# Transposing the first group of a row tile's exponentials ahead of the last multiplication of the tile before it

## The chip, the cores and the metric

One core of a Trainium2 chip runs the kernel. The metric is the device time of one execution in microseconds (us). Engines are named as in the profile: PE is the matrix engine (TensorE), PEld its weight loads, DVE the vector engine, ACT the scalar engine, POOL is GpSimd, SP the queue that starts most of the DMAs.

## What is computed

Two graph layers over 2708 nodes with 256 features. Only the attention of the first layer is touched by the change:

```python
for n in range(2):                        # STEPS
    probs = softmax((Xa @ W1.T @ W2.T) @ (Xa @ W3.T).T)
    mask  = the fewest largest probs of a row that sum to over 0.9
    A     = probs * mask;  A = A / A.sum(-1)
    Xf = R @ Xf                           # R: the given adjacency, with the identity added, by row sums
    Xa = A @ Xa
    Z  = Z + Xf @ U1[n].T + Xa @ U2[n].T
x = layernorm(x + (layernorm(x + Z) * g + b))
# then a second layer: masked attention with 4 heads, residual, layernorm
```

A is 2708 x 2708 and is never stored; it is made and used one row tile at a time.

## The kernel before

Rows are cut into 22 tiles, `rows = [128] * 16 + [110] * 6`. For a product A @ X the same 22 tiles are the blocks of the inner dimension, put into six `groups` of equal width: four groups of four tiles, and then one of four and one of two (the 110-wide ones).

For each of the two steps, `step` (L995) goes through the row tiles. A row tile t has its masked exponentials e (rows on partitions, 2708 columns) ready in the dictionary `ready`. `weigh` (L202) multiplies them by the current X. Since the inner dimension must lie on partitions, e is transposed first, group by group. `turned(n)` (L208) transposes up to four blocks on PE into a PSUM tile `tr` (L212) and copies it on ACT to an SBUF tile `eT` (L218). The multiplications of group n (L227) take eT as the stationary operand and add into one PSUM tile, `att`, of which there is one buffer (`ps_at`, bufs=1). Each fp32 multiplication is two matmul instructions in the profile, so a group of four blocks is 8 of them and the last group of two blocks is 4; a transpose is one. In the text below, "group 0" to "group 5" are these multiplications, and "the transposes of group n" their preparation.

`weigh` keeps one group ahead, within a row tile: it transposes group 0, and then for each n it transposes group n+1, multiplies group n, and calls `between(n)`. After the last group `between` (L1006) first reads `att` out with a scaled ACT copy into `xa` (L1010). Every `between` then calls `slot`.

A `slot` (L980) is the place where other work is woven in. It moves every search that is going on by one stage (`going`), starts a new one where `begin` says so, moves every piece of following work by one stage (`doing`), and then issues up to `spend` block multiplications of the two adjacency products R @ Xf (`walks`, L824, matmuls of L863). In step 0 `spend` is 0; in step 1 it is 7, 6, 7, 7, 6, 7 over the six groups.

A `search` (L811) makes e and its mask for one row tile. Its first stage issues the score matmuls of two of three column pieces (L631) and their exponentials on ACT (L635), the second stage the third piece. In step 0 it takes 6 stages. In step 1 it takes 13: stages 3 to 6 hold counts over e on ACT (L656), stage 7 a bound on DVE (L704 to L725), then come candidates, sorting and the replacement of ties, and the 13th masks e in place on DVE (L805). The search of tile t+3 is started in the slot after the last group of tile t, so that its 13th stage is issued in the slot right ahead of its own first transposes. There are three e buffers.

The stretch of code is under `tc.manual_schedule`: PE, ACT, DVE and POOL get their instructions in the order in which the Python code issues them. Between the steps there is a run of 13 slots, each with 7 block multiplications, which brings the searches of tiles 0, 1 and 2 of step 1 forward. The adjacency products have 968 block multiplications in all; the slots of step 1 and of that run issue up to as many, and what is issued in one slot is not left for a later one.

Of the kernel before, what the change touches and what calls it, by code (L numbers as in the profile page):

```python
# [8 lines left out]
F32 = mybir.dt.float32  # L9
# [7 lines left out]
P = 128  # L17
# [27 lines left out]
def kernel(  # L45
# [16 lines left out]
    nc = tc.nc  # L62
    N, D = x.shape
# [4 lines left out]
    NT = (N + P - 1) // P  # L68

    rows = [P] * 16 + [110] * 6  # L70
    assert sum(rows) == N and len(rows) == NT
    off = [sum(rows[:t]) for t in range(NT + 1)]
    chunks = [(c, min(CHUNK, N - c)) for c in range(0, N, CHUNK)]
    HT = NT // 2
    groups = []
# [29 lines left out]
    ident = const.tile([P, P], F32, name="ident")  # L105
# [67 lines left out]
    def share(g, tr):  # L173

        span, m = spans[g], rows[spans[g][0]]
        k = len(span) * H
        nc.tensor.transpose(
            tr[:k, 0, :m],
            s_src[:m, span[0] : span[-1] + 1, :].rearrange("p t h -> p (t h)"), ident[:m, :m],
        )  # L180
        nc.scalar.activation(line[:k, :m], tr[:k, 0, :m], AF.Exp, scale=1.0 - NEG_SLOPE)
        nc.sync.dma_start(shared[g], line[:k, :m])
# [16 lines left out]
            for _ in range(2)  # L199
        ]  # L200

    def weigh(acc, e, m, value, pool, ps, copies, between=None):  # L202

        def turned(n):  # L208
            grp = groups[n]
            tr = ps.tile([P, 4, P], F32, name="tr")  # L210
            for q, t in enumerate(grp):
                nc.tensor.transpose(  # L212
                    tr[: rows[t], q, :m], e[:m, off[t] : off[t + 1]], ident[:m, :m]
                )
            eT = pool.tile([P, 4, P], F32, name="eT")
            copy = copies[n % len(copies)]
            k = rows[grp[0]]
            copy(eT[:k, : len(grp), :m], tr[:k, : len(grp), :m])  # L218
            return eT

        ahead = turned(0)
        for n, grp in enumerate(groups):
            eT = ahead
            if n + 1 < len(groups):
                ahead = turned(n + 1)
            for q, t in enumerate(grp):
                nc.tensor.matmul(  # L227
                    acc, eT[: rows[t], q, :m], value(t),
                    start=(t == 0), stop=(t == NT - 1),
                )  # L230
            if between:
                between(n)


    def general_layer0():
        with ExitStack() as l0:
# [25 lines left out]
            tpp = l0.enter_context(tc.tile_pool(name="tpp", bufs=4))  # L262
            adjp = l0.enter_context(tc.tile_pool(name="adjp", bufs=2))
            ps_lg = l0.enter_context(tc.tile_pool(name="ps_lg", bufs=2, space=PSUM))
            ps_tr = l0.enter_context(tc.tile_pool(name="ps_tr", bufs=2, space=PSUM))
# [34 lines left out]
            def scores(s, t):  # L300

                m = rows[t]
                lo, hi = s * DA, (s + 1) * DA
                e = ep.tile([P, N], F32, name="e")
                for c0, w in chunks:
                    lg = ps_lg.tile([P, CHUNK], F32, name="lg")
                    nc.tensor.matmul(
                        lg[:m, :w], qT[lo:hi, off[t] : off[t + 1]], kT[lo:hi, c0 : c0 + w],
                        start=True, stop=True,
                    )  # L310
                    nc.scalar.copy(e[:m, c0 : c0 + w], lg[:m, :w])
                nmx = small.tile([P, 1], F32, name="nmx")
                nc.vector.tensor_reduce(nmx[:m], e[:m], axis=AX.X, op=ALU.max, negate=True)
                z = small.tile([P, 1], F32, name="z")
                nc.scalar.activation(e[:m], e[:m], AF.Exp, bias=nmx[:m], accum_out=z[:m])
                tau = small.tile([P, 1], F32, name="tau")
                nc.vector.tensor_scalar(tau[:m], z[:m], TOP_P, None, op0=ALU.mult)
                return e, tau
# [89 lines left out]
            def attend(t, e, rden, cur, dst):  # L408

                m = rows[t]  # L410
                ac = ps_ac.tile([P, CHUNK], F32, name="ac")
                weigh(ac[:m, :D], e, m, lambda j: cur[: rows[j], j, 0:D],
                      tpp, ps_tr, [nc.scalar.copy])
                nc.scalar.activation(dst, ac[:m, :D], AF.Copy, scale=rden[:m])

            def walk(s, t, dst):
# [52 lines left out]
            for s in range(STEPS):  # L469
                cur = xe if s == 0 else xa1  # L470
                ahead = scores(s, 0)
                for t in range(NT):
                    m = rows[t]
                    e, tau = ahead
                    if t + 1 < NT:
                        ahead = scores(s, t + 1)
# [6 lines left out]
                    rden = top_p(t, e, tau)  # L483
# [10 lines left out]
    def fast_layer0(ep, adjp):  # L494
# [3 lines left out]
        heldp, finp, rowp, w0, keep, sortp, tpp, wk = (  # L498
            l0.enter_context(tc.tile_pool(name=name, bufs=bufs))
            for name, bufs in (  # L500
                ("heldp", HELD), ("finp", 2), ("rowp", 2), ("w0", 1), ("keep", 1),
                ("sortp", 1), ("tpp", 3), ("wk", 1),
            )
        )
        ps_lg, ps_wk, ps_at, ps_tr = (
            l0.enter_context(tc.tile_pool(name=name, bufs=bufs, space=PSUM))
            for name, bufs in (("ps_lg", 2), ("ps_wk", 1), ("ps_at", 1), ("ps_tr", 2))
        )
# [69 lines left out]
        tr = ps_tr.tile([P, 4, P], F32, name="tr")  # L578
# [3 lines left out]
        for c in range(DC):  # L582
            tr = ps_tr.tile([P, 4, P], F32, name="tr")
# [227 lines left out]
        def search(s, t):  # L811

            e, z, tau = yield from scores(s, t)
            if s:
                seen = yield from survey(t, e, z, tau)
                src, rest = bound(t, e, z, tau, *seen)
            else:
                src, rest = e, tau
            yield
            cand = yield from candidates(s, t, src)  # L820
            yield
            ready[t] = e, (yield from settle(s, t, e, cand, rest))
# [148 lines left out]
        ready, held = {}, {}  # L971
# [3 lines left out]
        def advance(parts):  # L975
            for g in list(parts):
                if next(g, parts) is parts:
                    parts.remove(g)

        def slot(spend, begin=None):  # L980

            advance(going)
            if begin and begin[1] < NT:
                going.append(search(*begin))
                next(going[-1])
            advance(doing)
            owed[0] += spend
            while owed[0] > 0:
                owed[0] -= 1
                if next(stream, True):  # L990
                    break

        ahead = []

        def step(s, cur, spend):  # L995
            for t in range(NT):
                m = rows[t]
                e, rden = ready.pop(t)
                ac = ps_at.tile([P, CHUNK], F32, name="att")
                if s and t == NT - 2:  # L1000
                    share(0, ps_tr.tile([P, 4, P], F32, name="tr"))
                if s and t == NT - 1:
                    ahead.extend(room(ep))
                    spread(0, ahead)

                def between(n):  # L1006
                    last = n == len(groups) - 1
                    if last:
                        xa = heldp.tile([P, D], F32, name="xa1")
                        nc.scalar.activation(xa[:m], ac[:m, :D], AF.Copy, scale=rden)  # L1010
                        if s and t in c3:
                            nc.gpsimd.dma_start(c3[t][:m], xa[:m])
                            stored.add(t)
                        elif s:
                            held[t] = xa
                        else:
                            doing.append(after_attention0(t, xa))
                    slot(spend[n], (s, t + 3) if last else None)

                weigh(ac[:m, :D], e, m, lambda j: cur[: rows[j], j, 0:D],  # L1020
                      tpp, ps_tr, [nc.scalar.copy], between)

        def layer1_weights():

# [26 lines left out]
        for grp in groups:  # L1051
            k = rows[grp[0]]
# [13 lines left out]
        with tc.manual_schedule(engines=engines):  # L1066
            for n in range(10):
                slot(0, (0, n // 4) if n in (0, 4, 9) else None)
                for t in range(n * NT // 10, (n + 1) * NT // 10):
                    terms1(t, x_turned[:, :, off[t] : off[t + 1]])  # L1070
            layer1_weights()
            step(0, xm, [0] * len(groups))
            while doing:
                slot(SPEND_BETWEEN)


            for t in range(3):
                for n in range(6):
                    slot(SPEND_BETWEEN, None if n else (1, t))
                    if t == 2:  # L1080
                        break
            step(1, ba, SPEND_1)
            owed[0] = 0
            while doing:
                slot(NT)
# [234 lines left out]
```

## Time and profile before

| | |
|---|---|
| median of 3 runs | 1656.84 us (1656.59 to 1657.43) |
| the profiled execution: time, span | 1657.21 us, 1655.3 us |
| step 0 of the attention, by the first and last multiplications of it | 78 to 468 us |
| run of slots between the steps | 468 to 530 us |
| step 1 | 530 to 1252 us |
| last following work of layer 0, and layer 1 | 1252 to 1655 us |
| PE busy over the span | 1577.3 us, 95% |
| DVE, ACT, POOL busy | 74%, 45%, 26% |

A row of the costliest groups gives line, engine, operation, what it writes and reads, and the count; then the busy time, the mean length of one in ns, and the idle time of its engine just before it with what ended that. A row of the timeline gives the start, the length of a merged run of equal instructions, and in square brackets the idle time before it with its releaser. A row of the waits gives who waited for whom: us in total, times, and the longest.

### The profile page before, as it was taken

The page shows a single profiled execution, that of the slowest core. Times are in us where ns is not written, and L with a number is a line of the kernel's source. Part 1 is how long each engine was busy: PE and PEld are TensorE (multiplying, and loading weights), DVE is VectorE, ACT ScalarE, POOL GpSimd, SP SyncE. Part 2 cuts the span into 40 slices and gives each one's busy share as a digit, 9 for nine tenths or more (in the row PEclk, how much of TensorE's full clock was granted, in tenths as well). Part 3 has the DMA queues.
Part 4 walks back from the last instruction along what each step waited for, and adds up shares of the span by engine and source line. Part 5 has one row for each costly group of instructions (what it writes and reads, how often), then busy time and mean ns, then how long its engine had stood idle before and what let it go on. Part 6 is the DMA issues. An engine that isn't in the chain of part 4 may idle for free. (4 is left out here: it accounts for less than half of the span.)

```text
span 1655.3 us, 23835 instructions
## 1 busy us (share of the span) xinstructions
PE 1577.3 (95%) x8029; PEld 1035.8 (63%) x8029; DVE 1229.6 (74%) x3682; ACT 742.3 (45%) x1263; POOL 430.1 (26%) x908
## 2 busy tenths in 40 slices
PE   7999999999999999999999999999997999999894
PEld 3476667666677887787778877887773222222332
DVE  3676667666508877876888888987873999899795
ACT  3433444343335555455455655556524344243231
POOL 2200000000022223222225554455433030420313
PEclk9999999999999999999999999999997999999997
DMA  7200000000024333233333433433354333432231
GB/s 196 69 9 15 9 9 11 9 9 8 12 68 121 90 90 98 80 83 78 80 90 97 111 106 99 111 100 91 90 132 143 109 92 97 123 88 80 79 84 32
DMA packets 172493, 128.26 MB, mean 77 GB/s; under 512 B 44342, under 2 KB 161804, under 8 KB 172362
## 3 DMA queue, kind: packets, MB, share of 16 engines
q1 hardware_dynamic: 166442, 115.87, 26.0%
q0 software_dynamic: 3648, 9.26, 1.8%
q10 hardware_dynamic: 2272, 1.52, 0.3%
q8 instruction: 65, 1.06, 0.3%
q14 instruction: 66, 0.54, 0.1%
HBM read 111.78 MB, written 13.46 MB: 76 GB/s over the span
## 5 line engine op out<-in xcount | busy, mean ns | idle before, releaser
L218 ACT COPY eT<-tr 128x512 f32<-128x512 f32 (+5 forms) x264 | 137.7, 539 | 252.0 <-PE tr L212 251.5
L227 PE MATMUL att<-xm,eT 128*128 128x256 f32 (+3 forms) x968 | 229.3, 381 | 17.4 <-ACT eT L218 17.4
L656 ACT ACTIVATE junk<-e,minus,rth 128x2708 bf16<-128x2708 f32 (+1 forms) x88 | 232.8, 2646 | 14.6 <-POOL rth L688 13.7
L227 PE MATMUL att<-ba,eT 128*128 128x256 f32 (+3 forms) x968 | 232.9, 381 | 5.1 <-ACT eT L218 4.9
L1241 PE MATMUL acc<-pt,v 128*64 128x512 f32 (+3 forms) x1056 | 229.3, 555 | 5.7 <-DVE pt L1233 4.5
L863 PE MATMUL walk<-xe,blk 128*128 128x257 f32 (+3 forms) x968 | 223.8, 382 | 1.9 <-DVE xf L877 1.8
L863 PE MATMUL walk<-xm,blk 128*128 128x256 f32 (+3 forms) x968 | 221.8, 380 | 0.0
L1233 DVE SCALAR_TENSOR_TENSOR pt<-e,tj,blk 128x1024 f32<-128x1024 f32 (+3 forms) x176 | 186.5, 1117 | 29.3 <-PE acc L1248 12.5
L863 PEld LDWEIGHTS walk<-xe,blk 128*128 128x128 f32 (+3 forms) x968 | 177.3, 185 | 46.7 <-issue 13.7
L227 PEld LDWEIGHTS att<-xm,eT 128*128 128x128 f32 (+3 forms) x968 | 171.2, 186 | 44.7 <-ACT eT L218 22.2
L863 PEld LDWEIGHTS walk<-xm,blk 128*128 128x128 f32 (+3 forms) x968 | 177.8, 186 | 32.9 <-issue 4.9
L227 PEld LDWEIGHTS att<-ba,eT 128*128 128x128 f32 (+3 forms) x968 | 171.0, 186 | 32.6 <-ACT eT L218 10.2
L635 ACT ACTIVATE e<-lg 128x1024 f32<-128x1024 f32 (+1 forms) x132 | 121.0, 921 | 131.6 <-PE lg L631 131.3
L736 DVE MAX8 cand<-e 128x8 f32<-128x170 f32 (+1 forms) x352 | 89.7, 323 | 114.4 <-ACT e L635 114.3
L1241 PEld LDWEIGHTS acc<-pt,v 128*64 128x64 f32 (+1 forms) x1056 | 72.8, 138 | 158.3 <-issue 112.0
L212 PEld LDWEIGHTS tr<-ident,e 128*128 128x128 f32 (+3 forms) x968 | 113.6, 139 | 45.5 <-PE lg L631 14.5
L212 PE MATMUL tr<-ident,e 128*128 128x128 f32 (+3 forms) x968 | 139.4, 270 | 0.9 <-DVE e L805 0.5
L1171 ACT ACTIVATE blk<-blk 128x1024 f32<-128x1024 f32 (+3 forms) x66 | 63.1, 956 | 165.9 <-DMA blk<-in_adjT_dram 159.5
L1248 PE MATMUL acc<-pt,sb 128*32 128x512 f32 (+3 forms) x1056 | 123.6, 548 | 0.0
L1233 DVE SCALAR_TENSOR_TENSOR pt<-r,tj,blk 128x1024 f32<-128x1024 f32 (+1 forms) x88 | 110.6, 1314 | 8.2 <-issue 5.5
L736 DVE MAX8 cand<-scr 128x8 f32<-128x97 f32 (+1 forms) x616 | 101.7, 244 | 0.0
L877 DVE TENSOR_TENSOR xf<-walk,xe 128x257 f32<-128x257 f32 (+1 forms) x22 | 9.4, 426 | 112.4 <-PE walk L863 112.4
(197 smaller groups left out, 1941.0 us busy)
## 6 DMA issues: line engine op xcount, KB each, us to landing
blk<-in_adjT_dram SPq DMA_DIRECT2D x32, 704.0 KB
blk<-in_adjT_dram SPq DMA_DIRECT2D x32, 512.0 KB
blk<-in_adjT_dram SPq DMA_DIRECT2D x48, 330.0 KB
blk<-in_adjT_dram SPq DMA_DIRECT2D x32, 320.0 KB
blk<-in_adjT_dram SPq DMA_DIRECT2D x12, 605.0 KB
blk<-in_adjT_dram SPq DMA_DIRECT2D x12, 440.0 KB
blk<-in_adjT_dram SPq DMA_DIRECT2D x18, 283.6 KB
c<-cs POOLq DMA_DIRECT2D x32, 128.0 KB, 2.0
```

The costliest lines, as they stand in the source:

```text
L212: nc.tensor.transpose(tr[: rows[t], q, :m], e[:m, off[t] : off[t + 1]], ident[:m, :m])
L218: copy(eT[:k, : len(grp), :m], tr[:k, : len(grp), :m])
L227: nc.tensor.matmul(acc, eT[: rows[t], q, :m], value(t), start=(t == 0), stop=(t == NT - 1),)
L635: nc.scalar.activation(halves[:m, :, c0 : c0 + w], lg[:m, :, :w], AF.Exp, accum_out=zp[:m, n : n + 1],)
L656: nc.scalar.activation(junk[:m], e[:m], func, scale=rth, bias=minus1[:m], accum_out=acc)
L736: nc.vector.max(cand[:, n, :], src[:m, n * size : min(N, (n + 1) * size)])
L863: nc.tensor.matmul(ac[:m, :w], blk[: rows[j], j - j0, :m], cur[: rows[j], j, 0:w], start=(j == 0), stop=(j == NT - 1),)
L877: nc.vector.tensor_add(xf[:m], ac[:m, : D + 1], xe[:m, t, :])
L1171: nc.scalar.activation(bar, bar, AF.Sign)
L1233: nc.vector.scalar_tensor_tensor(pt[:k, :gw], r[h // 2][:k, h % 2, :gw], tj[:k, j, h : h + 1], mask, op0=ALU.max, op1=ALU.mult,)
L1241: nc.tensor.matmul(acc[h // 2][c][q * FO : (q + 1) * FO, :w], v[j][:k, h - 1 + q, :], pts[h - 1 + q][:k, c0 : c0 + w], **at,)
L1248: nc.tensor.matmul(acc[2][c][h * 32 : (h + 1) * 32, :w], sb[:k, j, h : h + 1].to_broadcast([k, 32]), pts[h][:k, c0 : c0 + w], **at,)
```

## The change

`turned` is taken out of `weigh` and becomes a function of its own that is given the e tile. `weigh` is given the transposed first group instead of making it, asks a function `turn_next` for each next group, and returns the one it got last. In `step`, `turn_next(6)` of tile t is group 0 of tile t+1. So the four transposes of that group and their copy are issued ahead of the multiplications of group 5 of tile t, not after the slot that follows these. Because e of tile t+1 must then be ready one slot earlier, every search starts one slot earlier (after group 4), and the run of slots between the steps has two slots more. The version of the first layer that is only run for inputs that the fast one can't do (`general_layer0`) is adapted and keeps its order.

```diff
-    def weigh(acc, e, m, value, pool, ps, copies, between=None):
-        def turned(n):
...
-        ahead = turned(0)
+    def turned(e, m, n, pool, ps, copy):
+        grp = groups[n]
+        tr = ps.tile([P, 4, P], F32, name="tr")
+        for q, t in enumerate(grp):
+            nc.tensor.transpose(
+                tr[: rows[t], q, :m], e[:m, off[t] : off[t + 1]], ident[:m, :m]
+            )
+        eT = pool.tile([P, 4, P], F32, name="eT")
+        k = rows[grp[0]]
+        copy(eT[:k, : len(grp), :m], tr[:k, : len(grp), :m])
+        return eT
+
+    def weigh(acc, ahead, m, value, turn_next, between=None):
         for n, grp in enumerate(groups):
-            eT = ahead
-            if n + 1 < len(groups):
-                ahead = turned(n + 1)
+            eT, ahead = ahead, turn_next(n + 1)
             for q, t in enumerate(grp):
                 nc.tensor.matmul(
                     acc, eT[: rows[t], q, :m], value(t),
...
             if between:
                 between(n)
+        return ahead
...
         def step(s, cur, spend):
+            first = None
             for t in range(NT):
                 m = rows[t]
-                e, rden = ready.pop(t)
+                e, rden = ready[t]
...
-                    slot(spend[n], (s, t + 3) if last else None)
-
-                weigh(ac[:m, :D], e, m, lambda j: cur[: rows[j], j, 0:D],
-                      tpp, ps_tr, [nc.scalar.copy], between)
+                    slot(spend[n], (s, t + 3) if n == len(groups) - 2 else None)
+
+                def turn_next(n):
+                    u = t + n // len(groups)
+                    if u == NT:
+                        return None
+                    return turned(ready[u][0], rows[u], n % len(groups), tpp, ps_tr, nc.scalar.copy)
+
+                first = weigh(
+                    ac[:m, :D], first or turn_next(0), m,
+                    lambda j: cur[: rows[j], j, 0:D], turn_next, between,
+                )
+                ready.pop(t)
...
             for t in range(3):
                 for n in range(6):
                     slot(SPEND_BETWEEN, None if n else (1, t))
-                    if t == 2:
+                    if (t, n) == (2, 2):
                         break
```

More of the change, by code (lines that the diff above doesn't have):

```diff
@@ L200, in room @@
         ]
-    def weigh(acc, e, m, value, pool, ps, copies, between=None):
-        def turned(n):
[L209 to L219, printed above, removed]
-        ahead = turned(0)
+    def turned(e, m, n, pool, ps, copy):
[10 more added lines that the diff above has]
+    def weigh(acc, ahead, m, value, turn_next, between=None):
         for n, grp in enumerate(groups):
-            eT = ahead
-            if n + 1 < len(groups):
-                ahead = turned(n + 1)
+            eT, ahead = ahead, turn_next(n + 1)
             for q, t in enumerate(grp):
@@ L411, in attend @@
                 ac = ps_ac.tile([P, CHUNK], F32, name="ac")
-                weigh(ac[:m, :D], e, m, lambda j: cur[: rows[j], j, 0:D],
-                      tpp, ps_tr, [nc.scalar.copy])
+                def turn_next(n):
+                    return turned(e, m, n, tpp, ps_tr, nc.scalar.copy) if n < len(groups) else None
+                weigh(ac[:m, :D], turn_next(0), m, lambda j: cur[: rows[j], j, 0:D], turn_next)
                 nc.scalar.activation(dst, ac[:m, :D], AF.Copy, scale=rden[:m])
@@ L1017, in between, with turn_next @@
                             doing.append(after_attention0(t, xa))
-                    slot(spend[n], (s, t + 3) if last else None)
-                weigh(ac[:m, :D], e, m, lambda j: cur[: rows[j], j, 0:D],
-                      tpp, ps_tr, [nc.scalar.copy], between)
+                    slot(spend[n], (s, t + 3) if n == len(groups) - 2 else None)
+                def turn_next(n):
+                    u = t + n // len(groups)
[7 more added lines that the diff above has]
+                ready.pop(t)
         def layer1_weights():
```

## The prediction

> **What bounds the kernel now.** I read the busy times by stage first, then PE's waits in each stage, then the timeline of PE where a row tile ends and the next begins. The windows give the stretch, its length, and busy time of PE, PEld, DVE, ACT, POOL, then the granted clock.
>
> ```profile
> 78.00:468.00 390.00, 371.70 (x1851) 269.48 (x1850) 249.76 (x920) 155.17 (x356) 31.66 (x95) 1.00 0.03 10
> ...
> 530.00:890.00 360.00, 357.20 (x1733) 286.36 (x1732) 282.12 (x1070) 192.75 (x243) 96.15 (x232) 1.00 0.33 87
> 890.00:1252.00 362.00, 359.14 (x1780) 289.23 (x1779) 299.21 (x1072) 198.21 (x379) 176.79 (x350) 1.00 0.39 103
> 1252.00:1275.00 23.00, 10.64 (x32) 5.53 (x32) 13.19 (x18) 10.14 (x38) 11.12 (x13) 0.59 0.55 166
> ```
>
> PE sets the pace of both steps: it is idle for 18.3 of 390 us in step 0 and 5.7 of 722 us in step 1, while DVE has 36% and 20% to spare. PE's waits in 78 to 468 us, and then in 530 to 1252 us:
>
> ```profile
> PE att L227 <- ACT eT L218: 17.4, 21, 1.0
> ```
> ```profile
> PE att L227 <- ACT eT L218: 4.9, 20, 0.4
> ```
>
> Nearly all the idle time is one wait, once per row tile: a multiplication waits for the ACT copy of its transposed group. PE's timeline shows which one (step 0, then step 1):
>
> ```profile
> 201.30 1.99 PE L631 MATMUL lg<-junk,qT 64*128 64x512 f32 x8
> 203.22 1.09 PE L212 MATMUL tr<-ident,e 128*128 128x128 f32 x8
> 205.18 1.99 PE L227 MATMUL att<-xm,eT 128*128 128x256 f32 x8 [0.87 <-ACT eT L218]
> 207.10 0.82 PE L631 MATMUL lg<-junk,qT 64*128 64x330 f32 x4
> ...
> 208.13 0.60 PE L212 MATMUL tr<-ident,e 128*128 128x128 f32 x4
> 208.57 1.89 PE L227 MATMUL att<-xm,eT 128*128 128x256 f32 x8
> 210.30 1.88 PE L922 MATMUL tr<-u_sb,xT 128*128 128x512 f32 x4
> ...
> 216.57 2.76 PE L227 MATMUL att<-xm,eT 110*128 110x256 f32 x12
> 219.25 1.99 PE L631 MATMUL lg<-junk,qT 64*128 64x512 f32 x8
> ```
> ```profile
> 819.60 1.02 PE L227 MATMUL att<-ba,eT 110*128 110x256 f32 x4
> 820.55 1.99 PE L631 MATMUL lg<-kT,qT 64*128 64x512 f32 x8
> ...
> 826.91 1.04 PE L212 MATMUL tr<-ident,e 128*128 128x128 f32 x8
> 828.18 1.99 PE L227 MATMUL att<-ba,eT 128*128 128x256 f32 x8 [0.24 <-ACT eT L218]
> 830.11 0.83 PE L631 MATMUL lg<-kT,qT 64*128 64x330 f32 x4
> ```
>
> The run of eight transposes is groups 0 and 1 of the new tile, with nothing else to cover the copy of group 0; everywhere else four transposes are followed by eight multiplications without a gap. ACT's timeline says why the wait is longer in step 0:
>
> ```profile
> 202.53 1.02 ACT L635 ACTIVATE e<-lg 128x1024 f32<-128x1024 f32 x1 [0.66 <-PE lg L631]
> ...
> 203.55 1.02 ACT L635 ACTIVATE e<-lg 128x1024 f32<-128x1024 f32 x1
> ...
> 204.54 1.07 ACT L218 COPY eT<-tr 128x512 f32<-128x512 f32 x2
> ...
> 219.36 0.47 ACT L1010 ACTIVATE xa<-att,rden 128x256 f32<-128x256 f32 x1 [2.17 <-PE att L227]
> ```
>
> The two exponentials of the search that this slot starts stand ahead of the copy. In step 1 the slot's block multiplications follow the scores, so they are done by then and only the copy itself shows.
>
> **What the Trainium skill says.** "Perfetto Trace Analysis", section Tensor Engine Instruction: PE's end times are estimated. The trace agrees (the transposes at 208.13 are 0.60 long, the next run starts 0.44 later), so I count from start to start, not the gaps. "TensorE: Matmul & The Clock Gate", Step-by-step: matmuls keep program order, only weight loads are drawn ahead; the trace shows no L227 passed by later work, so each entry's wait stops all behind it. The same page, What's actually happening: PE falls to half clock after an idle window of about 3.4 us. The waits are under 1 us and the clock is 1.00 in both steps (0.59 only in 1252 to 1275), so filling them wins no clock. "PSUM — Partial Sum Buffer", Engine vs sequencer instructions: ScalarE's queue is strictly in order; the copy at 204.54 starts at the end of the second exponential, as it says.
>
> **The change part by part.** *Entry, step 0.* Before, from the starts: groups 4 and 5 together take 219.25-216.57 = 2.68, the scores 203.22-201.30 = 1.92, eight transposes with group 0 and its wait 207.10-203.22 = 3.88; sum 8.48. After, the order is group 4, scores, four transposes, group 5, third score piece, four transposes, group 0. Four transposes take 208.57-208.13 = 0.44, a free group of eight 210.30-208.57 = 1.73, a group 5 alone ahead of scores 820.55-819.60 = 0.95, which is 0.08 over half of 1.73; I add this 0.08 to group 4 also, as scores now follow it. So 1.81+1.92+0.44+0.95+0.44+1.73 = 7.29 (the third piece is the same in both). The gain is 1.19 us, for the 19 entries whose slots start a search (tiles 1 to 19): 22.6. The entries of tiles 20 and 21 have no scores; their wait is small (0.29 of idle time at each in PE's timeline) and 0.3 each is taken: step 0 gives 23.2.
>
> *Entry, step 1.* Before: group 4 1.73, group 5 0.95, eight transposes with group 0 830.11-826.91 = 3.20; sum 5.88. After: 1.81+0.95+0.44+0.44+1.73 = 5.37. Scores and block multiplications are the same. The gain is 0.51, for 20 entries 10.2; tile 21's, where the mask is late by 0.5 today, 0.3. Step 1 gives 10.5. The first tile of each step keeps its wait.
>
> *What is late next: the read-out.* `att` has one buffer, so group 0 also waits for xa, now with four transposes less between; behind group 0 all of PE would queue. Count from the start L of the scores in step 0. ACT's exponentials end at L+3.24 (204.54-201.30), the copy of the next group 0 takes 0.59 (591 ns, mean of its group; L+3.83), and xa follows, 0.47: L+4.30. PE is back for group 0 at 1.92+0.44+0.95+0.76+0.44 = L+4.51 (0.76 is the third piece, 207.10 to 207.86 in PE's timeline). So 0.2 is spare: priced at nothing, with 0.3 x 19 = 6 us as the other end if ACT runs half a microsecond late. In step 1 seven block multiplications (about 3 us) lie between as well; no cost. The copy itself now has group 5, the third piece and four transposes of cover, 2.1 us; the next copy (group 1) follows the third exponential and has all of group 0, 1.7 us.
>
> *The searches one slot earlier.* All stages move together: PE's scores, ACT's counts, POOL's small steps, DVE's passes; each queue holds the same work in nearly the same order, and no DMA is added. What counts is that the mask is done at the entry.
>
> ```profile
> 820.41 3.02 DVE L805 SCALAR_TENSOR_TENSOR e<-scr,fact,e 128x2708 f32<-128x2708 f32 x1
> ```
>
> It ends at 823.43, and PE reads e at 826.91: 3.5 us spare. From the slot before to the entry PE now has the two transposes of group 5 (about 0.22) and the multiplications of group 4 (1.73) where it had group 5 (0.95), so 1.0 more. Cost nothing; queued behind a late mask would be the whole of PE.
>
> *Two more slots.* 14 block multiplications come before step 1 and are missing in its last tile: the sum of PE's work is the same. Gain or loss: at most 2 us either way (DVE waits in that run are 1.8 us today; the last tile has less to fill with, but its copies lie under 1.73 of multiplication). Zero.
>
> *The end of layer 0.* 1252 to 1275 is a chain that starts from the last xa. It moves as a whole, and layer 1 behind it; within 2 us either way as finishing work falls into other slots. Zero.
>
> *Sum.* 23.2+10.5 = 33.7. I keep back 1.5 for the small spare at the read-out: 32.2. The profiled execution took 1657.21 (its span of 1655.3 and 1.9 around it), 0.4 over the median, which is within the runs shown. 1657.2-32.2 = 1625.0.
>
> **Rivals.** *Only part (15%).* Either the read-out becomes the releaser in step 0, or the shorter runs cost more at each change of operation than I read. The gaps as the profile counts them are 17.4+4.9 = 22.3, which gives 1635; the read-out 0.5 us late (0.3 waited, 19 times) gives 1631. For it: 0.2 us of spare is little. Against: no work of ACT in the code stands between the copy and xa in step 0.
>
> *No change (3%).* The wait returns elsewhere, for instance DVE becomes the limit: 1657. Against: DVE has 36% and 20% spare. That the order is not kept is as good as excluded, since the timeline follows the code.
>
> *Slower (5%): the read-out behind the exponentials.* If ACT reached xa only after all three exponentials of a search (1.02+1.02+0.72 from ACT's timeline), it would come 2.8 us late, of which 0.2 is spare: 2.6 x 19 = 49 us in step 0, against a gain of 33.7: 1672. It decides from 2.0 us late (1.8 x 19 = 34). For it: strict order on ACT and one `att` buffer. Against: xa is issued ahead of the third, and the first two are fed by scores that PE now runs before group 5.
>
> **How the numbers follow.** As forecast, 1620 to 1630: 75%, with the two bounds of 2 us each and the read-out. Part of it: 15%. Better than 1620: 2%. No change 3%, slower 5%. The range from 1619 to 1637 leaves about 1 in 10 out, and what I have not thought of. About 0.2% (3.3 us) is what a measurement of this kernel can tell from no change: faster 0.92, same 0.03, slower 0.05.
>
> **What would show it.** PE's waits in step 0 should hold almost nothing for eT (the two first tiles' entries at most), and no new row "PE att <- ACT xa" of more than a microsecond or two; the timeline should read 8, scores, 4 transposes, 4, scores, 4 transposes, 8. Step 0 should last about 367 us, the run between the steps some 6 us longer (14 block multiplications, 0.43 each) and step 1 some 17 shorter. A wait of transposes for DVE e L805, several times, would make the searches' step wrong; a longer 1252 to 1275 stretch the end's.

## The result, and the profile after

| | before | after |
|---|---|---|
| median of 4 runs each, us | 1657.01 (1656.59 to 1657.43) | 1627.03 (1626.03 to 1628.40) |
| profiled execution: time, span | 1657.21, 1655.3 | 1626.46, 1624.7 |
| PE busy over the span | 1577.3 us | 1566.4 us |

The ratio is 0.982, with a 95% interval of 0.9803 to 0.9837. The change makes the kernel 30.0 us faster; the forecast was 32.2 us and a time of 1625.0.

The stages, from the starts of PE's matmuls in the two traces. A step goes from the start of its first multiplication to the start of its last, and the run between the steps ends where the first transposes of step 1 start. From there to step 1's first multiplication it is 1.3 us in both kernels, which no row holds.

| stage | before | after | change |
|---|---|---|---|
| to the first multiplication of step 0 | 78.9 | 78.6 | -0.3 |
| step 0 | 389.1 | 367.1 | -21.95 |
| run of slots between the steps | 62.1 | 74.6 | +12.5 |
| step 1 | 721.2 | 703.8 | -17.4 |
| end of layer 0, to layer 1's first multiplication | 21.7 | 18.4 | -3.3 |
| layer 1 | 381.0 | 380.8 | -0.2 |
| sum | | | -30.6 |

PE's waits in step 0 of the kernel after (who waited for whom, us in total, times, longest), and below in step 1:

```profile
PE tr L603 <- ACT qT L608: 0.5, 1, 0.5
PE att L225 <- ACT xa L1013: 0.4, 2, 0.2
PE tr L207 <- ACT xe L916: 0.3, 1, 0.3
```
```profile
PE walk L865 <- DVE xw L938: 0.7, 1, 0.7
PE att L225 <- ACT eT L212: 0.2, 1, 0.2
```

The waits for eT, 17.4 and 4.9 us before, are gone but for the first tile's entry in step 1. The row of the read-out is there, with 0.4 us and twice, at the two entries without scores. No transposes wait for a mask. PE's timeline at an entry of step 0 shows the new order:

```profile
191.58 1.89 PE L225 MATMUL att<-xm,eT 110*128 110x256 f32 x8
193.41 1.99 PE L633 MATMUL lg<-junk,qT 64*128 64x512 f32 x8
195.32 0.66 PE L207 MATMUL tr<-ident,e 128*128 128x128 f32 x4
195.82 1.03 PE L225 MATMUL att<-xm,eT 110*128 110x256 f32 x4
196.78 0.83 PE L633 MATMUL lg<-junk,qT 64*128 64x330 f32 x4
197.53 0.66 PE L207 MATMUL tr<-ident,e 128*128 128x128 f32 x4
198.03 1.89 PE L225 MATMUL att<-xm,eT 128*128 128x256 f32 x8
```

The run of eight transposes is now two runs of four with group 5 and the third score piece between. ACT's timeline at the same entry:

```profile
195.64 1.02 ACT L637 ACTIVATE e<-lg 128x1024 f32<-128x1024 f32 x1
...
196.64 0.58 ACT L212 COPY eT<-tr 128x512 f32<-128x512 f32 x1
197.10 0.50 ACT L1013 ACTIVATE xa<-att,rden 128x256 f32<-128x256 f32 x1
197.67 0.72 ACT L637 ACTIVATE e<-lg 128x660 f32<-128x660 f32 x1
```

The copy of group 0 still starts only when the second exponential has ended, 196.64, which is 1.3 us after its transposes began; PE does not need it before 198.03. The read-out ends at 197.60, so 0.43 us are spare, where the forecast had 0.2.

The stage that went against the forecast is the one between the steps. PE's timeline at its end, kernel after:

```profile
507.95 0.83 PE L633 MATMUL lg<-kT,qT 64*128 64x330 f32 x4
511.94 8.61 PE L865 MATMUL walk<-xe,blk 128*128 128x257 f32 x32 [3.16 <-DVE xf L879]
520.38 1.04 PE L207 MATMUL tr<-ident,e 128*128 128x128 f32 x8
```

A new idle time of 3.16 us stands ahead of the block multiplications of the two added slots. DVE's timeline of the same stretch says what it waits for:

```profile
508.11 3.04 DVE L723 SCALAR_TENSOR_TENSOR scr<-e,hi 128x2708 f32<-128x2708 f32 x1
...
511.46 0.42 DVE L879 TENSOR_TENSOR xf<-walk,xe 128x257 f32<-128x257 f32 x1
```

`xf` (L879) reads a finished row tile of R @ Xf out of the one PSUM tile `walk`, and the next row tile can't begin before that. It stands on DVE behind the mask (L807, 3.04 us) and the bound (L723, 3.04 us) of two searches, issued ahead of it. Before, the same two passes stood there too. DVE's timeline of the kernel before, and PE's:

```profile
530.35 3.04 DVE L721 SCALAR_TENSOR_TENSOR scr<-e,hi 128x2708 f32<-128x2708 f32 x1
...
533.70 0.42 DVE L877 TENSOR_TENSOR xf<-walk,xe 128x257 f32<-128x257 f32 x1
```
```profile
530.09 1.04 PE L212 MATMUL tr<-ident,e 128*128 128x128 f32 x8
531.37 1.99 PE L227 MATMUL att<-ba,eT 128*128 128x256 f32 x8 [0.24 <-ACT eT L218]
533.29 0.82 PE L631 MATMUL lg<-kT,qT 64*128 64x330 f32 x4
534.18 4.18 PE L863 MATMUL walk<-xe,blk 128*128 128x257 f32 x18
```

There PE had the first transposes, the first group 0 and a score piece of step 1 to do meanwhile: cover. It came to the next row tile at 534.18, just when `xf` was done. Now 16 more block multiplications come ahead of these, and the first of them needs `walk` at once. The windows (start and end, length, busy time of PE, PEld, DVE, ACT and POOL, granted clock, DMA share, GB/s) show a second price:

```profile
511.40:514.80 3.40, 2.86 (x7) 2.32 (x8) 3.37 (x21) 2.54 (x2) 2.31 (x6) 0.50 0.11 29
514.80:520.30 5.50, 5.50 (x27) 4.80 (x26) 5.22 (x25) 0.58 (x2) 0.92 (x3) 1.00 0.21 50
```

PE is at half clock from 511.4 to 514.8, so for the first 2.9 us of its work after the idle time. The 32 matmuls take 8.44 us from start to start (520.38-511.94) where 32 at full clock take 6.97: 1.5 us are lost. The Trainium skill's page "TensorE: Matmul & The Clock Gate", section What's actually happening, gives about 3.4 us for the idle window after which the clock is halved. Here the idle time is 3.16 us as the profile counts it, with PE's ends estimated, and 3.59 from the last start to the next. Shorter ones were enough in early_only (2.89) and readout_late (2.08), shown below, so 3.4 us is no safe limit here.

### The profile page after: what moved, and what is told of

It is laid out like the page before. It is cut to its first block, busy times and chain, and to the rows that moved or that the text cites. A ratio compares the mean times of both kernels' runs of the same rounds, so it can differ in the third digit from the quotient of the medians.

```text
span 1624.7 us, 23853 instructions
## 1 busy us (share of the span) xinstructions
PE 1566.4 (96%) x8029; PEld 1033.3 (64%) x8029; DVE 1225.6 (75%) x3682; ACT 746.8 (46%) x1263; POOL 431.9 (27%) x908
## 5 line engine op out<-in xcount | busy, mean ns | idle before, releaser
L212 ACT COPY eT<-tr 128x512 f32<-128x512 f32 (+5 forms) x264 | 141.3, 536 | 285.6 <-PE tr L207 282.8
L658 ACT ACTIVATE junk<-e,minus,rth 128x2708 bf16<-128x2708 f32 (+1 forms) x88 | 232.8, 2646 | 18.4 <-POOL rth L690 17.4
L225 PEld LDWEIGHTS att<-ba,eT 128*128 128x128 f32 (+3 forms) x968 | 169.6, 186 | 21.7 <-ACT eT L212 0.5
L207 PE MATMUL tr<-ident,e 128*128 128x128 f32 (+3 forms) x968 | 147.1, 271 | 0.3 <-ACT xe L916 0.3
L879 DVE TENSOR_TENSOR xf<-walk,xe 128x257 f32<-128x257 f32 (+1 forms) x22 | 9.4, 427 | 109.7 <-PE walk L865 109.7
```

Source lines behind the costliest of these rows:

```text
L207: nc.tensor.transpose(tr[: rows[t], q, :m], e[:m, off[t] : off[t + 1]], ident[:m, :m])
L225: nc.tensor.matmul(acc, eT[: rows[t], q, :m], value(t), start=(t == 0), stop=(t == NT - 1),)
L658: nc.scalar.activation(junk[:m], e[:m], func, scale=rth, bias=minus1[:m], accum_out=acc)
L879: nc.vector.tensor_add(xf[:m], ac[:m, : D + 1], xe[:m, t, :])
```

## Experiments

**Theories.** The theory: the gain is the turn itself, the transposes and copy of group 0 lying under group 5 instead of in the open; both steps give their part independently, and the added slots cost some 5 us of it through the wait for `xf` and the half clock. The rivals: (1) the gain comes from the searches starting a slot earlier, which moves the exponentials away from the entry, and not from the turn; (2) one step gives it all, or the two depend on each other; (3) the 5 us between the steps are no loss, only work that step 1 would have had. Every edit below is against the kernel after, and none leaves out a part of the computation.

**The halves of the change.** *early_only*: searches a slot earlier and two slots more, but no transposes ahead.

```diff
-                    if u == NT:
+                    if u > t:
```

> Searches start one slot earlier and the run between the steps has two slots more, but the first group of a tile is transposed where it was before. Theory (the gain is the cover of the first copy): nearly no gain in step 0, since the third exponential now stands ahead of the copy in place of the other two; step 0 387 to 390 us from first to last multiplication (before 389.1, after 367.1), about 1655 to 1660 in all, the stall of the two more slots (4.5) included. Rival (the exponentials ahead of the copy were the cost, and starting the search earlier moves them away): step 0 some 13 us or more shorter, about 1645.

Measured: 1654.44 us, ratio 0.9985 (0.9978 to 0.9992). Slightly faster than before and 27 us slower than after. The total is 0.6 us under the range expected; step 0 is well under it: 380.4 us, 8.7 less than before. PE's and ACT's timelines at an entry show why:

```profile
201.56 1.09 PE L207 MATMUL tr<-ident,e 128*128 128x128 f32 x8
203.04 1.99 PE L225 MATMUL att<-xm,eT 128*128 128x256 f32 x8 [0.39 <-ACT eT L212]
```
```profile
201.70 0.72 ACT L637 ACTIVATE e<-lg 128x660 f32<-128x660 f32 x1 [0.17 <-PE lg L633]
...
202.41 1.06 ACT L212 COPY eT<-tr 128x512 f32<-128x512 f32 x2
```

Only the third, short exponential (0.72 us) is now ahead of the copy, where before it was two of 1.02. The wait shrinks from 0.87 to 0.39 us. So rival (1) holds for a part: 8.7 of the 21.95 us of step 0 come with the earlier searches alone, and the turn added to them gives the other 13.2. What the turn would give in step 0 without the earlier searches was not run. In step 1 the rival does not hold: from group 0 of one tile to group 0 of the next, the kernel after is about 0.5 us shorter than early_only in twenty of the 21 entries (32.38 and 32.88, for instance), and that is the turn's part. Step 1 of early_only is only 2.8 us shorter than before, though work of 7.8 us was moved out of it. PE's waits for eT there are 7.7 us in all against 4.9, most of the difference at one entry near the end:

```profile
1238.65 3.10 PE L225 MATMUL att<-ba,eT 128*110 128x256 f32 x8 [2.89 <-ACT eT L212]
```

From 1239.4 to 1242.8 PE is then at half clock, which costs some 1.6 us more; about half a microsecond of the difference stays unexplained.

*step0_only* and *step1_only* do the turn and the earlier searches in one step each; the first has no added slots.

```diff
-                    slot(spend[n], (s, t + 3) if n == len(groups) - 2 else None)
+                    slot(spend[n], (s, t + 3) if n == len(groups) - 2 + s else None)
...
-                    if u == NT:
+                    if u == NT or (u > t and s):
...
-                    if (t, n) == (2, 2):
+                    if (t, n) == (2, 0):
```
```diff
-                    slot(spend[n], (s, t + 3) if n == len(groups) - 2 else None)
+                    slot(spend[n], (s, t + 3) if n == len(groups) - 1 - s else None)
...
-                    if u == NT:
+                    if u == NT or (u > t and not s):
```

> The change in step 0 alone; step 1 and the run of slots ahead of it as before. Theory: step 0 as after (367 us), the run between the steps 62 and step 1 721 as before, the end of layer 0 as before (21.7); 1635. Rival (the steps are coupled, step 0's gain is given back later): over 1640.

> The change in step 1 alone, with the two more slots; step 0 as before. Theory: step 0 389, the run between the steps 74.6 with the stall of 3.2 us, step 1 704, the end of layer 0 18.4 as after; 1649, so that the two halves add to the whole. Rival (the end of layer 0 is shorter by chance of arrival): the end stays near 21.7 and the time is about 1652.

Measured: step0_only 1635.83 us, ratio 0.9874 (0.9857 to 0.9890), 20.8 below the kernel before of that comparison; step1_only 1648.18 us, ratio 0.9951 (0.9935 to 0.9968), 8.4 below. The sum is 29.2 of the 30.0 us: the halves add up, and rival (2) falls. Step 0 alone lasts 367.1 us, as in the kernel after, and step 1 alone 704.2.

**The added slots.** *slots_only* is the kernel before with two slots more and nothing else.

```diff
-                    slot(spend[n], (s, t + 3) if n == len(groups) - 2 else None)
+                    slot(spend[n], (s, t + 3) if n == len(groups) - 1 else None)
...
-                    if u == NT:
+                    if u > t:
```

> As before, with nothing of the change but the two more slots between the steps. Theory: these cost the wait of a block multiplication for DVE's xf (3.2 us) and half clock behind it (1.4), and bring the end of layer 0 from 21.7 to 18.4; step 0 389; about 1.2 us slower than before, 1658, with the run between the steps at 74.6 and the end at 18.4. Rival (the end is shorter because of the order of the tiles' transposes, not of the earlier block multiplications): the end stays at 21.7 and the time is 1661.

Measured: 1663.57 us, ratio 1.0042 (1.0027 to 1.0058): slower than before by 6.4 us, where 1.2 were expected. Block multiplications moved ahead of step 1 are thus not merely moved, and rival (3) falls. PE's timeline and the clock behind it:

```profile
534.38 10.27 PE L865 MATMUL walk<-xe,blk 128*128 128x257 f32 x32 [3.16 <-DVE xf L879]
```
```profile
534.00:542.00 8.00, 7.62 (x21) 6.18 (x22) 7.73 (x41) 3.12 (x3) 3.05 (x8) 0.59 0.12 33
```

The same 3.16 us of idle time, but here the half clock lasts 6.8 us (533.8 to 540.6) and costs 3.1: the 32 matmuls take 10.27 us where the kernel after needs 8.61. PE's waits for eT in step 1 are also 7.5 us in place of 4.9, 2.41 of it at one entry near the end. These two make up most of the miss.

*no_blocks_extra* keeps the two slots, but they add no block multiplications.

```diff
-                    slot(SPEND_BETWEEN, None if n else (1, t))
+                    slot(0 if t == 2 and n else SPEND_BETWEEN, None if n else (1, t))
```

> As after, but the two more slots issue no block multiplications (these are left to the slots of step 1 and the ones after it). Theory: the block multiplication that waits 3.2 us for DVE's xf, and the half clock of 1.4 us behind it, are covered by the first transposes and group 0 of step 1; 4.5 us less than after, 1622.5. Rival (the wait comes back at the first block multiplication of step 1 or in the masks of tiles 1 and 2): 1626 to 1629.

Measured: 1631.74 us, ratio 0.9854 (0.9837 to 0.9870): slower than after instead of 4 us faster. PE's timeline:

```profile
512.12 1.78 PE L865 MATMUL walk<-xe,blk 128*128 128x257 f32 x4 [3.17 <-DVE xf L879]
513.69 1.91 PE L207 MATMUL tr<-ident,e 128*128 128x128 f32 x8
```

The wait is still there. The slot before stops at the end of a row tile of R @ Xf with two of its seven blocks not yet issued, and these are owed to the next slot; so two block multiplications (4 matmuls) wait in the place of sixteen, and at half clock the eight transposes then take 1.91 us instead of 1.04. And the end of layer 0 lasts 21.6 us again, as before. The edit did not take the wait away, and so tells nothing of its price.

*pay_later* holds those two back also, and pays them in the first slots of step 1.

```diff
+                    owed[0] -= 30 if t == 2 and n else 0
                     slot(SPEND_BETWEEN, None if n else (1, t))
+                    owed[0] += 30 if t == 2 and n else 0
```

> As after, but in the two more slots no block multiplication is issued at all, and what they would have issued is due in the first slots of step 1. (In the run before on this, one that was still owed went into the slot and kept the wait, and the end of layer 0 got longer, since the rest came later.) Theory: the wait for xf is covered by the first transposes and group 0, and the end stays at 18.4: 4.5 us less than after, 1622.5. Rival (the wait moves to the first block of step 1 or to the masks of tiles 1 and 2): 1626 to 1629.

Measured: 1629.58 us, ratio 0.9836 (0.9823 to 0.9850): another miss. The wait for `xf` is gone, and the first group 0 of step 1 waits instead. PE's timeline, and ACT's:

```profile
516.39 3.77 PE L225 MATMUL att<-ba,eT 128*128 128x256 f32 x8 [6.11 <-ACT eT L212]
```
```profile
512.71 0.39 ACT L675 ACTIVATE rth<-slope,nguess,y 128x1 f32<-128x1 f32 x1 [2.60 <-POOL slope L671]
513.13 2.64 ACT L658 ACTIVATE junk<-e,minus,rth 128x2708 bf16<-128x2708 f32 x1
...
515.77 1.05 ACT L212 COPY eT<-tr 128x512 f32<-128x512 f32 x2
```

The copy stands on ACT behind a count of tile 2's search (2.64 us), which itself waits for POOL. The block multiplications in the added slots had covered that. So these slots need something on PE, only not something that waits for `xf`.

*five_at_15*, *five_at_12*, *six_at_15* leave the slots as they are and issue five or six more block multiplications earlier in the run between the steps, so that the end of the R @ Xf row tile comes at another place in DVE's queue. The first and third put them into the sixth slot of tile 1 (n = 5), the second into the third (n = 2). The diff is six_at_15's; the others have 5 and (1, 5), and 5 and (1, 2).

```diff
+                    owed[0] += 6 if (t, n) == (1, 5) else 0
                     slot(SPEND_BETWEEN, None if n else (1, t))
```

> As after, with five more block multiplications due in the last slot ahead of tile 2's first, so that the row tile of the product ends one slot earlier and DVE's xf for it is queued ahead of the mask of tile 0 and the bound of tile 1. The slots keep their block multiplications, so that ACT's counts stay covered. Theory: the wait of 3.2 us and the half clock of 1.6 us behind it are gone, the rest stays: the run between the steps about 72 us with five more blocks in it, 1622 in all. Rival (whatever is freed there is waited for at the next end of a row tile, in the first slots of step 1): 1626 to 1629.

> The same five blocks, due three slots earlier. Theory: two ends of row tiles move by a slot, and the wait of 1.3 us behind the sorting of tile 0 is gone too; 1621. Rival: the earlier ends meet other DVE passes and wait there; 1624 to 1627.

> As the run with five more blocks due in the last slot ahead of tile 2's first, with six. There the wait of 3.2 us was gone, but the next end of a row tile fell on the first block of step 1's first slot, and 2.2 us were waited for it one slot later. With one block more it falls on the last block ahead of step 1, and the first transposes and group 0 lie behind it as cover. Theory: that wait goes too; 2 us less than with five, about 1622.5. Rival (DVE's passes in that place are long enough to be waited for wherever the end falls): 1625 again.

Measured: five_at_15 1624.77 us, ratio 0.9811 (0.9798 to 0.9825); five_at_12 1627.94, 0.9826 (0.9812 to 0.9839); six_at_15 1622.26, 0.9791 (0.9778 to 0.9804). With five in slot 5 the wait of 3.16 us and the half clock are gone, but at the next row tile's end, already in step 1, a new one of 2.21 us stands. With five in slot 2 several small waits (1.27, 0.59 and 2.22 us for `xf`, 1.57 for eT) take back nearly all of it. With six that row tile ends with the last block before step 1, as PE's timeline shows:

```profile
512.55 6.35 PE L865 MATMUL walk<-xe,blk 128*128 128x257 f32 x28
518.75 1.04 PE L207 MATMUL tr<-ident,e 128*128 128x128 f32 x8
520.02 1.99 PE L225 MATMUL att<-ba,eT 128*128 128x256 f32 x8 [0.24 <-ACT eT L212]
```

Its `xf` runs under the transposes and group 0. The 28 matmuls take 6.2 us from start to start, 0.22 each: full clock. The run between the steps takes 72.6 us with 2.6 us more work in it, and the whole kernel is 4.8 us faster than the kernel after. These two were not timed side by side; their runs (1621.66 to 1622.97 and 1626.03 to 1628.40) lie apart while the kernels before beside them agree (1657.10 and 1657.01). This agrees with the price read from the trace: 3.2 us idle and 1.5 us of half clock.

**The next gate.** *readout_late* lets ACT read `att` out four times in step 0 (the copies are equal), to test the rival of the prediction that ended slower.

```diff
-                        nc.scalar.activation(xa[:m], ac[:m, :D], AF.Copy, scale=rden)
+                        for _ in range(1 if s else 4):
+                            nc.scalar.activation(xa[:m], ac[:m, :D], AF.Copy, scale=rden)
```

> As after, but in step 0 the read-out of the accumulator is issued four times over on ACT, so that its last one ends about 1.4 us later. Theory: after has 0.35 to 0.4 us to spare between the read-out and group 0 of the next tile; 1.0 us is waited at 19 entries and 1.4 at two, 22 us: 1649, in waits of att for xa. Rival (PE is held by the copies alone): 1627 to 1629.

Measured: 1656.93 us, ratio 1.0000 (0.9991 to 1.0008): 1.5 us more of ACT's time per tile takes back the whole gain. PE's waits in step 0, then its timeline:

```profile
PE att L225 <- ACT xa L1014: 22.5, 21, 1.7
```
```profile
207.24 1.99 PE L225 MATMUL att<-xm,eT 128*128 128x256 f32 x8 [0.99 <-ACT xa L1014]
```

Step 0 lasts 394.3 us, 27.1 more than in the kernel after, for 22.5 us of shown waiting; I had expected less. The run of slots after it is 3.5 us longer too, since the last tile's read-out is late as well:

```profile
475.94 0.63 PE L616 MATMUL tr<-ident,xa 110*128 110x110 f32 x2 [2.08 <-ACT xa L1014]
476.36 4.69 PE L865 MATMUL walk<-xe,blk 128*128 128x257 f32 x14
```

In the kernel after that wait is 0.56 us, and the same 14 matmuls take 3.22; here PE is at half clock from 475.9 to 479.3. The mechanism of that rival is real: group 0 waits for the read-out as soon as it is 0.4 us late. What excluded the rival is that `xa` is issued ahead of the third exponential.

## Why the prediction was right

By its own terms, from the profiled executions (- is faster):

| term | forecast | measured |
|---|---|---|
| entries of step 0 | -23.2 | -21.95 |
| entries of step 1 | -10.5 | -9.7 |
| two more slots, net of moved work | 0 (2 either way) | +4.8 |
| end of layer 0 | 0 (2 either way) | -3.3 |
| kept back for the read-out | +1.5 | nothing lost there |
| ahead of step 0, and layer 1 | 0 | -0.5 |
| sum | -32.2 | -30.6 |

**Step 0: right.** Counting from the scores' start L (193.41 after), the forecast had PE back for group 0 at L+4.51 and the read-out done at L+4.30; measured are L+4.62 and L+4.19. The mis-sized piece is the transposes: four of them behind score matmuls take 0.50 from start to start (195.82-195.32 and 198.03-197.53), not the 0.44 of four behind other multiplications. That is 0.12 less gain per entry. Half of it comes back where the forecast did not look: the two transposes of `xa` (L616) no longer stand behind a score piece and take 0.22 (199.97-199.75) in place of 0.28 (L614, 226.12-225.84 before). From group 0 of one tile to group 0 of the next, the 19 entries gain 1.13 on average, against 1.19, which is 21.5 us; the two without scores give 0.4. What the forecast did not separate is that 8.7 of the stage's 21.95 come already with the earlier searches (early_only).

**Step 1: right.** The stage is 17.4 us shorter. Of this, 16 block multiplications of 0.4355 us (7.0) and a third score piece (0.8) have only moved ahead of it; 9.7 remain, about 0.5 per entry. The forecast moved 14 blocks and no score piece; two blocks owed from the slot before come with them, as PE's matmuls of the block multiplications ahead of step 1 show (252 after, 220 before).

**Two more slots: the step that failed.** The prediction counted the work of PE as moved and bounded the rest by 2 us, because DVE's waits in that run had been 1.8 us. It asked how much PE would wait there today and not what would wait if other work came first. The stage grew by 12.5: 7.0 of blocks, 0.8 of scores, 3.2 waiting and 1.5 of half clock. slots_only shows the cost by itself, six_at_15 that it can be had back.

**End of layer 0: the other wrong zero, in our favour.** PE waits there for a chain of finishing work. ACT's timeline of the kernel before, where the chain starts, and the same read-out after:

```profile
1252.31 1.06 ACT L1171 ACTIVATE blk<-blk 128x1024 f32<-128x1024 f32 x1 [1.74 <-DMA blk<-in_adjT_dram]
...
1253.50 1.06 ACT L1176 ACTIVATE blk<-blk 128x1024 f32<-128x1024 f32 x1
1254.45 0.47 ACT L1010 ACTIVATE xa<-att,rden 110x256 f32<-110x256 f32 x1
```
```profile
1225.90 0.47 ACT L1013 ACTIVATE xa<-att,rden 110x256 f32<-110x256 f32 x1 [1.42 <-PE att L225]
```

Before, the last `xa` stood on ACT behind two preparations of layer 1 and started about 1.5 us after PE's last multiplication (group 5 starts at 1251.95 and takes 1.03); after, ACT was idle and took it at once. From `xa` to layer 1's first multiplication it is 1274.29-1254.45 = 19.84 before and 1243.86-1225.90 = 17.96 after. Every run whose added slots issue their blocks, or pay them soon after, has the short end (18.4 in early_only, slots_only, step1_only, pay_later and the three with five or six more); those that don't, step0_only and no_blocks_extra, have 21.9 and 21.6. So it goes with the blocks being done earlier and not with the turn. Which piece of the tail's finishing work moved for the second part of it was not tested alone.

The two wrong zeros, +4.8 and -3.3, largely cancel, and so do the reserve and the smaller gain of the entries. The mechanism in both steps was forecast as it came; that the total is only 2.2 us off is in part luck.

## What to carry to other kernels

A copy is hidden only if the work put ahead of its reader on PE is longer than all that stands ahead of it in the copying engine's own queue; count that queue, not the copy. Filler work is not neutral either: where it accumulates in a single PSUM buffer, its read-out stands in another engine's queue, and two more slots of it can turn a covered pass into an idle PE. When moving filler, look where its accumulations end, and put those ends ahead of work that needs nothing from them.

## What the runs showed of the hardware

By the granted clock in the traces, some idle times of PE were followed by a stretch of half clock, and its length came in steps of 3.4 us: 3.4 in the kernel after and 6.8 in slots_only for the same idle time of 3.16 us (1.5 and 3.1 us lost), and 17.1 and 23.9, five and seven times as long, at the end of layer 0 in the kernels after and before. Its start is not tied to the idle time: in slots_only it begins 0.6 us before PE goes on (533.8, then 534.4), in step1_only 1.4 us after that (533.9, then 535.4). Nor did the length of the idle time alone decide: 2.89 us in early_only and 2.08 in readout_late were followed by half clock, 2.41 in slots_only and 2.21 in five_at_15 were not. What decides was not tested.

Four transposes of 128 columns directly behind score matmuls (64 rows) took 0.49 us from start to start in step 0 of the kernel after, and 0.44 behind the other matmuls. Why was not tested.

An entry that waits costs more than the profile's gap: 22.5 us of waiting at 21 entries in readout_late cost 27.1 us, about 0.2 more for each. Where a wait only got shorter, this did not come back: in early_only the waits of step 0 fell from 17.4 to 7.9 us, and the step gained 8.7.
